# Local attention: softmax weights divided before they are turned, outputs made with features on partitions

## The chip, the cores and the metric

The kernel runs on one core of a Trainium2 chip. The core has TensorE (PE in the profile; its weight loads are a row of their own, PEld), VectorE (DVE), ScalarE (ACT), GpSimd (POOL) and SyncE (SP, which here only issues DMAs). Each engine works through its own queue in order, and semaphores make one wait for another. TensorE's results go to PSUM, from which DVE and ACT read them; everything else lies in SBUF. The metric is the device time of one execution in microseconds.

## The reference

The program is a stack of two adaLN blocks on an input of 4 batches x 1024 tokens x 128 features, each block with an attention and a feed-forward part, all in float32. The second block's feed-forward part is itself a small transformer of two layers with local attention, and it is what the change touches. Of it this matters:

```python
q, k, v = split(shift_token(x) @ wqkv)           # 8 heads of 64
q, k = l2norm(q) * qs, l2norm(k) * ksc
q, k = rotary_xpos(q, k)
bq = q.reshape(b, h, w, 64, d) * 8.0             # windows of 64 queries
bk, bv = look_around(k), look_around(v)          # 128 keys: the window before and this one
sim = einsum('bhwid,bhwjd->bhwij', bq, bk)
sim = where((i < j) | (i > j + 64) | (j == -1), -max, sim)
attn = softmax(sim, axis=-1)
out = einsum('bhwij,bhwjd->bhwid', attn, bv)
x = x + out @ wo
x = x + (a * gelu(g)) @ w2 + b2                  # after a layer norm and x @ w1
```

## The kernel before, in words

Earlier stages (the first block, the second block's windowed attention) fill the first 668 us or so and are not touched. The last stage, from line 786 on, makes the small transformer: 2 layers x 4 batches x 8 tiles of 128 tokens, 64 tiles in one loop, `g` counting them. A tile holds two windows of 64 queries. Features lie on partitions for the residual stream (`yT`, `xT`, `hs`), tokens for everything between the projections and the turned weights.

The work on a tile is spread over several rounds of the loop:

- `project` (L796, two rounds ahead): one matmul each for q and k (`qk`), the squares and their sums (`sq` on ACT, `ss` on DVE), the rotary products `co` and `si` on DVE, and on POOL `co + si` (L819), the inverse norm by a power (L818) and, for k, its product (L821).
- `turn` (L824, one round ahead): four transposes of q or k (`qktr`), copied to `qT` by ACT (L832) or into the batch's `kT` by DVE (L838).
- `values` (L840): v = h @ wv, copied by ACT (L847) to a tile of 8 heads x 65 columns whose last column POOL sets to one (L846); two DMAs of 64 partitions each make `ve`, the same values one window earlier.
- `scores` (L856): the mask goes into PSUM by a matmul (L863), the scores of the tile are added (L873), DVE takes the negative maxima (L877) and scales them by q's inverse norm (L878), and ACT writes exp (L882), eight instructions of 128 columns, with scale and bias as per-partition operands. The `j` of all these functions is a head's half: head 2c + j.
- `flip` (L885, one round later): four transposes of the weights per `j` (`ptr`, L890), copied to `pt` by ACT (L892).
- `outputs` (L895, two rounds later), per `j`: eight matmuls of 65 columns with the turned weights as the stationary operand (L903). Column 64 is the sum of the exps, by the column of ones. DVE takes its reciprocal (L905) and multiplies the 64 feature columns by it (L908). Queries are on partitions.
- `back` (L910, three rounds later): four transposes (L916) put features on partitions, and ACT copies them to `os` (L920).
- `project_out` (L922): every four tiles, `os` times `wo`, added to `yT` by DVE (L928).

The MLP of an earlier group of four tiles is cut into side jobs (L947 to L981: shift, layer norm in and out, gate, up, down) that a table hands to particular rounds. A gate, an up or a down job is three matmuls of 512 columns.

PE's queue is written by hand: the loop at the end of the stage calls these functions in the order in which PE is to do them. The other engines' queues are put in order by the framework's scheduler. PSUM has two banks for scores (`pS`) and six for everything else (`pM`); a matmul into one of the six waits until the last reader of what lay there is done. `pr` and `pt` have four buffers each.

Of the kernel before, what the change touches and what calls it, by code (L numbers as in the profile page):

```python
# [19 lines left out]
F32 = mybir.dt.float32  # L20
BF16 = mybir.dt.bfloat16
AF = mybir.ActivationFunctionType
ALU = mybir.AluOpType
# [3 lines left out]
P = 128  # L27
B, N, D = 4, 1024, 128
NT = N // P
BLK = 512  # L30
# [6 lines left out]
HEADS, DH, DEPTH = 8, 64, 2  # L37
# [11 lines left out]
def adaln_blocks(ctx: ExitStack, tc: tile.TileContext, a: dict, out: bass.AP):  # L49
    nc = tc.nc  # L50
    pe, act, dve, pool = nc.tensor, nc.scalar, nc.vector, nc.gpsimd
# [4 lines left out]
    def const(name, shape, dtype=F32):  # L56
        return cp.tile(shape, dtype, tag=name, name=name)
# [5 lines left out]
    def bc(ap, shape):  # L63

        return ap.unsqueeze(len(ap.shape)).to_broadcast(shape)
# [35 lines left out]
    ident = const("ident", [P, P])  # L101
# [10 lines left out]
    with tc.tile_pool(name="modps", bufs=2, space=PSUM) as mp:  # L112
        sc = const("sc", [P, 2, B])
        act.activation(sc, cT, AF.Silu)
        for blk in range(2):
            ps = mp.tile([P, 6, B], F32, tag="mod", name=f"modps{blk}")
# [92 lines left out]
    ps = both.enter_context(tc.tile_pool(name="ps", bufs=1, space=PSUM))  # L209
# [94 lines left out]
    with (  # L304
# [7 lines left out]
        kept = {}  # L312
# [325 lines left out]
    with (  # L638
# [61 lines left out]
        def outputs(b, t):  # L700

            O = ps.tile([P, 4, P], F32, tag="o", name=f"o_{b}_{t}")
            kept1["go"] = O
            for x in range(2):
                for g in range(2):
                    pe.matmul(
                        O[64 * g : 64 * g + 64, x, :], lhsT=hm64 if x else kept1[b, "vg"][:, g, :], rhs=kept1[b, t, "pg"][:, g, :],
                        start=(x == 0), stop=False, skip_group_check=True,
                    )
            cs = [c for c in range(4 * t - 2, 4 * t + 4) if c >= 0]  # L710
            for c in cs:
                lo, hi = max(c * KB, t * P), min(c * KB + W3, (t + 1) * P)
                for x in range(2):
                    for j in range(4):
                        pe.matmul(  # L715
                            O[32 * j : 32 * j + 32, x, lo - t * P : hi - t * P],
                            lhsT=hm32 if x else kept1[b, c // 4, "v"][:, 4 * (c % 4) + j, :],
                            rhs=kept1[b, c // 4, "p", j][:, c % 4, lo - c * KB : hi - c * KB],
                            start=False, stop=(c == cs[-1]), skip_group_check=True,
                        )  # L720
            if t % 4 == 0:
                kept1[b, t // 4, "os"] = wb.tile([P, BLK], F32, tag="os", name=f"os_{b}_{t}")
            os = kept1[b, t // 4, "os"]
            rs = wp.tile([P, P], F32, tag="rs", name=f"rs_{b}_{t}")
            dve.reciprocal(rs, O[:, 1, :])
            dve.tensor_tensor(os[:, (t % 4) * P : (t % 4 + 1) * P], O[:, 0, :], rs, ALU.mult)
# [24 lines left out]
        def when(g, f, *args):  # L751
            if 0 <= g < NG8:
                f(*divmod(g, NT), *args)

        for g in range(NG8 + 2):
            b, t = divmod(g, NT)
# [30 lines left out]
    with (  # L787
# [6 lines left out]
        kept = {}  # L794
# [45 lines left out]
        def values(l, b, t):  # L840

            nt = f"{l}_{b}_{t}"
            ps = pM.tile([P, BLK], F32, tag="mid", name=f"v_{nt}")
            pe.matmul(ps, lhsT=hs[l, b][:, t * P : (t + 1) * P], rhs=wl[l][0][:, 2, :], start=True, stop=True)  # L844
            v = wp.tile([P, HEADS, DH + 1], F32, tag="v", name=f"vs_{nt}")
            pool.memset(v[:, :, DH : DH + 1], 1.0)  # L846
            act.copy(v[:, :, 0:DH], ps.rearrange("p (h e) -> p h e", e=DH))  # L847
            ve = wp.tile([P, HEADS, DH + 1], F32, tag="ve", name=f"ve_{nt}")
            if t == 0:
                pool.memset(ve[0:64], 0.0)  # L850
            else:
                nc.sync.dma_start(out=ve[0:64], in_=kept[l, b, t - 1, "v"][64:128])
            nc.sync.dma_start(out=ve[64:128], in_=v[0:64])
            kept[l, b, t, "v"], kept[l, b, t, "ve"] = v, ve

        def scores(l, b, t):  # L856

            nt = f"{l}_{b}_{t}"
            q, k = kept[l, b, t, "q"], kept[l, b, "k"]
            S = [pS.tile([P, 4, P], F32, tag="s", name=f"s_{nt}_{j}") for j in range(2)]  # L860
            for j in range(2):
                rw = slice(64 * j, 64 * j + 64)
                pe.matmul(S[j], lhsT=rep64[rw, :], rhs=mkl[rw, :].unsqueeze(1).to_broadcast([64, 4, P]), start=True, stop=False)  # L863
            if t == 0:
                for j in range(2):
                    rw = slice(64 * j, 64 * j + 64)
                    pe.matmul(S[j][0:64, :, 0:64], lhsT=rep64[rw, 0:64], rhs=neg64[rw, :].unsqueeze(1).to_broadcast([64, 4, 64]), start=False, stop=False)
            for c in range(4):
                for e in range(2):
                    for j in range(2):  # L870
                        rw, qs = slice(64 * j, 64 * j + 64), slice(64 * e, 64 * e + 64)
                        at = (2 * t + e) * 64
                        pe.matmul(S[j][qs, c, :], lhsT=q[rw, c, qs], rhs=k[rw, c, at : at + P], start=False, stop=(c == 3))  # L873
            mx = wp.tile([P, 2, 4], F32, tag="mx", name=f"mx_{nt}")
            rq = kept[l, b, t, "ss"][:, 0, :].rearrange("p (c j) -> p j c", j=2)
            for j in range(2):
                dve.tensor_reduce(mx[:, j, :], S[j], AX.X, ALU.max, negate=True)  # L877
                dve.tensor_tensor(mx[:, j, :], mx[:, j, :], rq[:, j, :], ALU.mult)  # L878
            for j in range(2):
                pr = wp.tile([P, 4, P], F32, tag="pr", name=f"pr_{nt}_{j}", bufs=4)  # L880
                for c in range(4):
                    act.activation(pr[:, c, :], S[j][:, c, :], AF.Exp, bias=mx[:, j, c : c + 1], scale=rq[:, j, c : c + 1])  # L882
                kept[l, b, t, "pr", j] = pr

        def flip(l, b, t, j):  # L885
# [6 lines left out]
            act.copy(pt, tp)  # L892
            kept[l, b, t, "pt", j] = pt

        def outputs(l, b, t, j):  # L895
            nt = f"{l}_{b}_{t}_{j}"
            pt = kept.pop((l, b, t, "pt", j))
            o = pM.tile([P, BLK], F32, tag="mid", name=f"o_{nt}")
            o = o[:, 0 : 4 * (DH + 1)].rearrange("p (h e) -> p h e", e=DH + 1)
            for c in range(4):  # L900
                for e, vv in ((0, kept[l, b, t, "ve"]), (1, kept[l, b, t, "v"])):
                    qs = slice(64 * e, 64 * e + 64)
                    pe.matmul(o[qs, c, :], lhsT=pt[:, c, qs], rhs=vv[:, 2 * c + j, :], start=True, stop=True)  # L903
            rs = wp.tile([P, 4, 1], F32, tag="rs", name=f"rs_{nt}", bufs=4)
            dve.reciprocal(rs, o[:, :, DH : DH + 1])  # L905
            if j == 0:
                kept[l, b, t, "o"] = wp.tile([P, 4, 2, DH], F32, tag="on", name=f"on_{nt}", bufs=2)
            dve.tensor_tensor(kept[l, b, t, "o"][:, :, j, :], o[:, :, 0:DH], rs.to_broadcast([P, 4, DH]), ALU.mult)  # L908

        def back(l, b, t):  # L910

            nt = f"{l}_{b}_{t}"
            on = kept.pop((l, b, t, "o"))
            tp = pM.tile([P, 4, P], F32, tag="mid", name=f"otr_{nt}")
            for c in range(4):
                pe.transpose(tp[:, c, :], on[:, c, :, :].rearrange("p j e -> p (j e)"), ident)  # L916
            i = t % 4
            if i == 0:
                kept[l, b, t // 4, "os"] = wb.tile([P, 4, BLK], F32, tag="os", name=f"os_{nt}")
            act.copy(kept[l, b, t // 4, "os"][:, :, i * P : (i + 1) * P], tp)  # L920

        def project_out(l, b, k):  # L922
            s = slice(k * BLK, (k + 1) * BLK)
# [78 lines left out]
        for l in range(DEPTH):  # L1002
            for b in range(B):
                g = (l * B + b) * NT
# [18 lines left out]
        for g in range(-2, tiles + 12):  # L1023
            side = steps.get(g, [])
            when(g, scores)
            when(g + 2, project, 0)
            when(g - 1, flip, 0)
            when(g + 2, project, 1)
            when(g - 1, flip, 1)
            when(g + 1, turn, 0)  # L1030
            when(g - 2, outputs, 0)
            for f, args in side[:1]:
                f(*args)
            when(g + 1, turn, 1)
            when(g - 2, outputs, 1)
            when(g, values)
            when(g - 3, back)

            f0 = g - 7 if g < tiles - 2 else g - 6
            if f0 % 4 == 0 and 0 <= f0 < tiles and g != tiles - 1:  # L1040
                project_out(f0 // (B * NT), f0 // NT % B, f0 % NT // 4)
            for f, args in side[1:]:
                f(*args)
# [148 lines left out]
```

## Time and profile before

| | us |
|---|---|
| median of 3 runs | 1399.29 (1398.83 to 1407.56) |
| the profiled execution | 1399.1 |
| its span on the core | 1397.3 |
| last stage's first score matmul for tile 0 | 669.2 after the span's start |
| eight tiles, 1087.41 to 1175.47 | 88.06 |

The page of the profile gives, for each engine, busy time with its share of the span and the number of instructions, and the groups of instructions by line with mean durations and with the idle time ahead of them. Matmuls are pipelined, so PE's busy time counts overlapping work once, and the distance between the starts of two matmuls tells more than their durations. A float32 matmul shows as two rows. The granted TensorE clock over the span is 0.982 of full speed, and 1.00 in the last stage from 700 us on.

### The profile page before, as it was taken

How to read it: one execution, taken by the hardware profiler on the slowest of the kernel's cores; microseconds unless marked ns; L12 is line 12 of the kernel's file. 1: busy time of each engine (PE TensorE's matmuls, PEld its weight loads, DVE VectorE, ACT ScalarE, POOL GpSimd, SP SyncE). 2: the span in 40 equal slices, each digit the busy share in tenths (PEclk: the TensorE clock that was granted, in tenths of full speed). 3: DMA queues.
4: the chain of work that ended last, by engine and by line, in shares of the span. 5: the costliest groups of instructions: out<-in, count | busy, mean ns of one | idle time of the engine just before them, and what ended most of it. 6: DMA issues, size and time to landing. Idle time of an engine off the chain costs nothing.

```text
span 1397.3 us, 33849 instructions
## 1 busy us (share of the span) xinstructions
PE 1311.6 (94%) x13908; PEld 810.3 (58%) x13908; DVE 885.1 (63%) x2090; ACT 702.8 (50%) x1453; POOL 730.6 (52%) x750
## 2 busy tenths in 40 slices
PE   5799988997999999998899999999999999999997
PEld 4544544444777677676466566656666566666553
DVE  5655444523555555554788778877788777887753
ACT  2463532321222222222576776767667776677752
POOL 4454537461232405211987676666767667766620
PEclk9799999998999999999899999999999999999999
DMA  6031221213000000000111111111211111111111
GB/s 180 0 123 55 68 67 57 69 53 121 3 3 3 17 3 18 3 3 3 24 33 45 38 43 32 24 43 33 48 34 25 43 32 43 44 35 36 40 35 30
DMA packets 38655, 56.14 MB, mean 40 GB/s; under 512 B 6331, under 2 KB 18661, under 8 KB 38373
## 3 DMA queue, kind: packets, MB, share of 16 engines
q1 hardware_dynamic: 37204, 52.44, 14.1%
q8 instruction: 110, 1.80, 0.5%
q10 hardware_dynamic: 1296, 1.54, 0.3%
q14 instruction: 45, 0.36, 0.1%
HBM read 27.24 MB, written 2.36 MB: 21 GB/s over the span
## 4 chain that ended last, share of the span: by engine, by line
PE 77%; DVE 8%; POOL 7%; ACT 3%; issue 3%; DMA 1%; POOLq 0%; ACTq 0%; SPq 0%
PE qk L802 7%; PE v L844 4%; PE o L903 4%; PE s L873 4%; PE t L677 4%; PE yp L927 4%; PE qktr L829 4%; PE ptr L890 3%; PE o L715 3%; PE gm L961 3%; PE h L494 3%; PE a L970 3%; PE ym L978 3%; PE vp L653 3%; POOL u L498 2%
## 5 line engine op out<-in xcount | busy, mean ns | idle before, releaser
L819 POOL TENSOR_TENSOR co<-co,si 128x512 f32<-128x512 f32 x128 | 162.7, 1273 | 129.1 <-DVE si L812 128.7
L818 POOL TENSOR_TENSOR ss<-ss,nhalf 128x16 f32<-128x16 f32 x64 | 187.2, 2925 | 4.7
L882 ACT ACTIVATE pr<-s,mx,ss 128x128 f32<-128x128 f32 x512 | 186.5, 480 | 1.8
L805 ACT ACTIVATE sq<-qk 128x512 f32<-128x512 f32 x128 | 79.5, 621 | 171.7 <-PE qk L802 98.1
L802 PE MATMUL qk<-wqkv,hs 128*128 128x512 f32 x256 | 137.2, 620 | 0.8 <-DVE xT L732 0.8
L498 POOL TENSOR_TENSOR u<-u,cw 128x512 f32<-128x512 f32 x64 | 81.1, 1270 | 93.2 <-ACT u L497 74.5
L494 PE MATMUL h<-hT,w 128*128 128x512 f32 x256 | 122.1, 597 | 1.6 <-DVE g L500 1.6
L877 DVE TENSOR_REDUCE mx<-s 128x4 f32<-128x512 f32 x128 | 82.3, 684 | 56.1 <-PE s L873 56.0
L500 DVE TENSOR_TENSOR g<-u,h 128x512 f32<-128x512 f32 x64 | 43.7, 685 | 114.8 <-POOL u L498 112.6
L285 DVE TENSOR_REDUCE mx<-s 128x4 f32<-128x448 f32 x128 | 70.9, 616 | 70.4 <-PE s L282 70.4
L680 ACT ACTIVATE pt<-t 128x384 f32<-128x384 f32 x128 | 55.8, 488 | 116.9 <-PE t L677 116.9
L650 POOL COPY hr<-hT 128x512 f32<-128x512 f32 x32 | 19.5, 614 | 176.4 <-PE vp L653 172.3
L807 DVE TENSOR_TENSOR co<-qk,ab 128x512 f32<-128x512 f32 x128 | 87.7, 685 | 28.6 <-ACT sq L805 28.3
L890 PEld LDWEIGHTS ptr<-ident,pr 128*128 128x128 f32 x512 | 63.6, 141 | 64.8 <-issue 53.4
L829 PE MATMUL qktr<-ident,co 128*128 128x128 f32 x512 | 78.1, 275 | 11.5 <-POOL co L821 10.5
L497 ACT ACTIVATE u<-h 128x512 f32<-128x512 f32 x64 | 38.3, 598 | 97.3 <-PE h L494 90.4
L903 PE MATMUL o<-vs,pt 128*64 128x65 f32 x1024 | 86.9, 228 | 0.0
L812 DVE TENSOR_TENSOR si<-qk,ab 128x512 f32<-128x512 f32 x128 | 86.8, 678 | 0.0
L903 PE MATMUL o<-ve,pt 128*64 128x65 f32 x1024 | 86.6, 227 | 0.0
L814 DVE TENSOR_REDUCE ss<-sq 128x8 f32<-128x512 f32 x128 | 86.2, 673 | 0.0
L494 PEld LDWEIGHTS h<-hT,w 128*128 128x128 f32 x256 | 47.8, 192 | 61.9 <-issue 53.5
L903 PEld LDWEIGHTS o<-ve,pt 128*64 128x64 f32 x1024 | 69.2, 137 | 23.1 <-issue 16.1
(234 smaller groups left out, 3060.6 us busy)
## 6 DMA issues: line engine op xcount, KB each, us to landing
cw<-cd SPq DMA_DIRECT2D x128, 128.0 KB, 3.1
ve<-vs SPq DMA_DIRECT2D x120, 130.0 KB, 2.3
hs_m<-hT SPq DMA_DIRECT2D x24, 128.0 KB, 2.2
xin<-in_x SPq DMA_DIRECT2D x4, 512.0 KB, 6.9
hs<-hT SPq DMA_DIRECT2D x8, 256.0 KB, 2.9
out<-out SPq DMA_DIRECT2D x8, 256.0 KB, 2.5
hs<-hT SPq DMA_DIRECT2D x8, 255.8 KB, 3.7
w<-in_w SPq DMA_DIRECT2D x3, 512.0 KB, 5.0
```

The lines of the kernel that those rows point to most:

```text
L494: pe.matmul(h, lhsT=w[:, c * P : (c + 1) * P], rhs=hT[b][:, blk(k)], start=True, stop=True)
L498: pool.tensor_tensor(u, u, kept[b, k, "cw"][:, c, :], ALU.mult)
L802: pe.matmul(ps, lhsT=hs[l, b][:, t * P : (t + 1) * P], rhs=wl[l][0][:, w, :], start=True, stop=True)
L807: dve.tensor_tensor(co, ph, abs_[l][:, 0, t, w, :].unsqueeze(1).to_broadcast([P, HEADS, DH]), ALU.mult)
L812: dve.tensor_tensor(si.rearrange("p h (i e) -> p h i e", i=2), ex, sn, ALU.mult)
L814: dve.tensor_reduce(ss[:, w, :], sq, AX.X, ALU.add)
L818: pool.tensor_tensor(ss, ss, nhalf[:, 0:2].unsqueeze(2).to_broadcast([P, 2, HEADS]), ALU.pow)
L819: pool.tensor_tensor(co, co, si, ALU.add)
L829: pe.transpose(tp[:, i, :], co[:, i * P : (i + 1) * P], ident)
L882: act.activation(pr[:, c, :], S[j][:, c, :], AF.Exp, bias=mx[:, j, c : c + 1], scale=rq[:, j, c : c + 1])
L890: pe.transpose(tp[:, c, :], pr[:, c, :], ident)
L903: pe.matmul(o[qs, c, :], lhsT=pt[:, c, qs], rhs=vv[:, 2 * c + j, :], start=True, stop=True)
```

## The change

The division by the sum of the exps moves from the outputs to the weights, ahead of their turning, and the outputs are made with the values as the stationary operand, so that their features come out on partitions.

- `values` makes tiles of 64 columns a head; the column of ones and its memset are gone.
- `scores` asks each exp for the sum along its row (`accum_out`), takes the reciprocals on DVE and multiplies the weights by them in place, per `j`.
- `outputs` makes both `j` in one call: 16 matmuls of 64 columns with `v` or `ve` as the stationary operand and the turned weights as the moving one, into one PSUM tile, which ACT copies to `os`.
- `back` is gone, and with it the four transposes of a tile.
- In the loop, the outputs stand after the first side job and ahead of the second `turn`. In the order that the scheduler makes for DVE, the two reciprocals and two products stand behind `ss` of the round's q projection and ahead of `co` of its k projection; the kT copy stands behind that projection in most rounds, and behind the first product in the rounds that hold `project_out`.

```diff
-            v = wp.tile([P, HEADS, DH + 1], F32, tag="v", name=f"vs_{nt}")
-            pool.memset(v[:, :, DH : DH + 1], 1.0)
-            act.copy(v[:, :, 0:DH], ps.rearrange("p (h e) -> p h e", e=DH))
-            ve = wp.tile([P, HEADS, DH + 1], F32, tag="ve", name=f"ve_{nt}")
+            v = wp.tile([P, HEADS, DH], F32, tag="v", name=f"vs_{nt}")
+            act.copy(v, ps.rearrange("p (h e) -> p h e", e=DH))
+            ve = wp.tile([P, HEADS, DH], F32, tag="ve", name=f"ve_{nt}")
...
+            sm = wp.tile([P, 2, 4], F32, tag="sm", name=f"sm_{nt}")
             for j in range(2):
                 pr = wp.tile([P, 4, P], F32, tag="pr", name=f"pr_{nt}_{j}", bufs=4)
                 for c in range(4):
-                    act.activation(pr[:, c, :], S[j][:, c, :], AF.Exp, bias=mx[:, j, c : c + 1], scale=rq[:, j, c : c + 1])
+                    act.activation(
+                        pr[:, c, :], S[j][:, c, :], AF.Exp, bias=mx[:, j, c : c + 1], scale=rq[:, j, c : c + 1], accum_out=sm[:, j, c : c + 1]
+                    )
+                dve.reciprocal(sm[:, j, :], sm[:, j, :])
+                dve.tensor_tensor(pr, pr, bc(sm[:, j, :], [P, 4, P]), ALU.mult)
                 kept[l, b, t, "pr", j] = pr
...
-        def outputs(l, b, t, j):
-            nt = f"{l}_{b}_{t}_{j}"
-            pt = kept.pop((l, b, t, "pt", j))
-            o = pM.tile([P, BLK], F32, tag="mid", name=f"o_{nt}")
-            o = o[:, 0 : 4 * (DH + 1)].rearrange("p (h e) -> p h e", e=DH + 1)
+        def outputs(l, b, t):
+
+            nt = f"{l}_{b}_{t}"
+            pt = [kept.pop((l, b, t, "pt", j)) for j in range(2)]
+            o = pM.tile([P, 4, P], F32, tag="mid", name=f"o_{nt}")
             for c in range(4):
                 for e, vv in ((0, kept[l, b, t, "ve"]), (1, kept[l, b, t, "v"])):
                     qs = slice(64 * e, 64 * e + 64)
-                    pe.matmul(o[qs, c, :], lhsT=pt[:, c, qs], rhs=vv[:, 2 * c + j, :], start=True, stop=True)
-            rs = wp.tile([P, 4, 1], F32, tag="rs", name=f"rs_{nt}", bufs=4)
-            dve.reciprocal(rs, o[:, :, DH : DH + 1])
-            if j == 0:
-                kept[l, b, t, "o"] = wp.tile([P, 4, 2, DH], F32, tag="on", name=f"on_{nt}", bufs=2)
-            dve.tensor_tensor(kept[l, b, t, "o"][:, :, j, :], o[:, :, 0:DH], rs.to_broadcast([P, 4, DH]), ALU.mult)
-
-        def back(l, b, t):
-
-            nt = f"{l}_{b}_{t}"
-            on = kept.pop((l, b, t, "o"))
-            tp = pM.tile([P, 4, P], F32, tag="mid", name=f"otr_{nt}")
-            for c in range(4):
-                pe.transpose(tp[:, c, :], on[:, c, :, :].rearrange("p j e -> p (j e)"), ident)
+                    for j in range(2):
+                        pe.matmul(o[64 * j : 64 * j + 64, c, qs], lhsT=vv[:, 2 * c + j, :], rhs=pt[j][:, c, qs], start=True, stop=True)
             i = t % 4
             if i == 0:
                 kept[l, b, t // 4, "os"] = wb.tile([P, 4, BLK], F32, tag="os", name=f"os_{nt}")
-            act.copy(kept[l, b, t // 4, "os"][:, :, i * P : (i + 1) * P], tp)
+            act.copy(kept[l, b, t // 4, "os"][:, :, i * P : (i + 1) * P], o)
...
             when(g + 1, turn, 0)
-            when(g - 2, outputs, 0)
             for f, args in side[:1]:
                 f(*args)
+            when(g - 2, outputs)
             when(g + 1, turn, 1)
-            when(g - 2, outputs, 1)
             when(g, values)
-            when(g - 3, back)
```

## The prediction

> **What bounds the kernel now.** I read the page first, then the busy time of one whole batch of the last stage (eight tiles), then the groups of that stage, then the timeline of single tiles.
>
> ```profile
> PE 1311.6 (94%) x13908; PEld 810.3 (58%) x13908; DVE 885.1 (63%) x2090; ACT 702.8 (50%) x1453; POOL 730.6 (52%) x750
> ...
> 1087.41:1175.47 88.06, 87.84 (x807) 53.43 (x807) 69.18 (x149) 61.36 (x132) 60.04 (x59) 1.00 0.16 36
> ```
>
> In the second line the columns are the stretch, its length, then busy time of PE, PEld, DVE, ACT, POOL, then granted clock. PE has work at every moment of the 88.06 us, DVE for 79% of them. Tiles come in a pattern of four, named here by their PE side job, with these distances between first score matmuls (L873): gate 10.5 (1131.80 to 1142.32), up 10.95 (1098.32 to 1109.27), down 10.52 (1109.27 to 1119.79), projection 12.01 (1119.79 to 1131.80). Their sum is 44.0; the stretch from 750 to 1344 holds 54 tiles at this pace. So PE's queue paces the stage. But how far behind is DVE? The last thing that a tile's scores need is the kT copy (L838), which DVE does at the end of its round:
>
> ```profile
> 1131.80 1.10 PE L873 MATMUL s<-kT,qT 64*64 64x128 f32 x32
> ...
> 1134.68 0.69 DVE L807 TENSOR_TENSOR co<-qk,ab 128x512 f32<-128x512 f32 x1 [0.24 <-ACT sq L805]
> ...
> 1138.46 0.69 DVE L807 TENSOR_TENSOR co<-qk,ab 128x512 f32<-128x512 f32 x1 [1.02 <-ACT sq L805]
> ...
> 1140.26 0.68 DVE L838 COPY kT<-qktr 128x512 f32<-128x512 f32 x1
> ```
>
> ```profile
> 1135.02 2.92 ACT L882 ACTIVATE pr<-s,mx,ss 128x128 f32<-128x128 f32 x8
> 1137.77 0.66 ACT L805 ACTIVATE sq<-qk 128x512 f32<-128x512 f32 x1
> 1138.24 0.66 ACT L892 COPY pt<-ptr 128x512 f32<-128x512 f32 x1
> ```
>
> Each line is a start, a length, and the instruction with what ended its engine's idle time. This is a gate tile. DVE's second co waits for sq, which stands behind the eight exps on ACT. kT ends at 1140.94, and the next scores start at 1142.32: 1.3 us to spare after 0.1 for the handing over. In the up tile kT ends at 1109.21 and the scores start at 1109.27: nothing to spare. In the down tile kT ends at 1119.27, scores start at 1119.79: 0.4 to spare.
>
> **What the change removes.** The groups of 750 to 1400 us (busy us and mean ns of one after the first bar):
>
> ```profile
> L882 ACT ACTIVATE pr<-s,mx,ss 128x128 f32<-128x128 f32 x440 | 160.3, 479 | 1.7
> ...
> L908 DVE TENSOR_TENSOR on<-o,rs 128x256 f32<-128x256 f32 x115 | 48.5, 421 | 3.4
> ...
> L916 PE MATMUL otr<-ident,on 128*128 128x128 f32 x232 | 34.9, 273 | 0.0
> ...
> L905 DVE RECIPROCAL rs<-o 128x4 f32<-128x4 f32 x114 | 19.7, 173 | 10.5 <-PE o L903 10.3
> ```
>
> PE loses four transposes (L916) a tile. Their place in the queue is 1107.98 to 1108.42, or 0.53 ahead of the masks: 0.44 to 0.53 us, so 64 x 0.5 = 32 us of PE. The output matmuls stay 16 of 64 columns instead of 65; one start of a group goes, under 0.1 us. DVE loses two reciprocals and two 128x256 multiplies, about 1.1 us of queue a tile, but they lie in holes: those of the first head half stand between ss and the wait for sq (1136.79 to 1137.43), those of the second half behind kT. Neither is ahead of kT on the path. POOL loses a 0.11 us memset from an idle stretch: nothing. The evacuation of v becomes contiguous (612 ns row, same size), and the os copy keeps its 620 ns; both free. What is moved: the first half's outputs go behind the first side job, with no DMA of theirs, and on ACT the os copy goes ahead of v's copy. That puts v 0.6 later, and v and its two DMAs (2.3 us) are read two tiles on: free, with some 20 us of cover.
>
> **What it adds.** (1) Two reciprocals (0.17, and 0.22 to the next start) and two 128x512 multiplies with both inputs in SBUF. The nearest row is L359, 0.67 to 0.69 us alone; back to back such instructions start every 0.60 to 0.65. The built order puts all four ahead of the second co, and in gate, up and down tiles kT stands behind that co, si and ss. (2) Accumulation in 512 exps. No row shows it. Summing can't shorten an exp, so from below nothing; from above the smallest ACT row, sc 128x8 at 209 ns, if each sum is an instruction of its own. Exps of 480 start every 0.35, so they overlap by 0.12 to 0.13, and such an instruction would add 0.08 to 0.21. [...] I take 0.09 each: 0.72 for eight. (3) The reciprocal waits for four exps and sits at the head of DVE's queue; co, si, ss, kT, and so PE's next scores, wait behind it.
>
> [...] A DVE multiply with both inputs in SBUF meets POOL:
>
> ```profile
> 880.23 1.04 POOL L821 TENSOR_TENSOR co<-co,ss 128x512 f32<-128x512 f32 x1
> ...
> 880.50 0.86 DVE L878 TENSOR_TENSOR mx<-mx,ss 128x4 f32<-128x4 f32 x2
> ```
>
> L878 takes 0.15 alone; here the first takes 0.79, ending with L821. At 166.32, L359 takes 1.43 beside L498. [...] the pair of L878 at 698.18 runs in 0.28 inside an L818 that lasts from 697.24 to 700.16. I go by the row: L819 (1.27), L821 (1.04) and L150 (1.04) block, L818 does not. [...]
>
> **Tile by tile**, in us from the tile's first score matmul.
> Gate: the exps end at 6.14 now, 6.86 then. The second multiply starts at 7.1, co at 7.75 instead of 6.66, kT ends at 10.2. PE, which lost 0.5, is later than that: the built waits let the output matmuls start only when the second pt copy has freed its PSUM bank (7.10, then 7.85), followed by 1.2 of outputs (now in one piece), 0.52 qktr, 0.96 v, 0.33 masks: 10.85. Cost +0.3 (-0.4 with free sums, +1.3 with 0.21).
> Up: the three ge of the MLP end on DVE at 7.9 (8.5 now: the matmuls start 0.6 earlier, no first outputs ahead of them). Then 0.65 + 0.2 + 0.65 of the new work, then co, si, ss, kT, 2.4 as now: scores at 11.9. Cost +0.95 (+1.7 with 0.21).
> Down: layer-norm work on DVE starts the round 0.55 earlier than now (the second multiply behind kT is gone). First multiply at 5.4, second ready at 7.2 when the exps are done; POOL's L149, L150, L819 run from 4.9 to 8.4, so it starts at 7.2 or behind L819 at 8.4. hT and kT follow: +0.6 or +1.8, I take +1.2.
> Projection: kT stands behind the first multiply only, but v now waits for that copy with nothing between qktr and v (outputs stood there): v at 7.4, yp at 8.4 against 8.16 now: +0.2 (+0.9 with 0.21).
> Sum: 2.65 per four tiles, x 13.5 = +36. The ten tiles before 750, where kT stands early and POOL's L821 paced the round, grow by about 0.6 each, as the first multiply waits for L819 there: +6. The profiled execution took 1399.1 (span 1397.3, 1.8 around it), within 0.2 of the median of the runs. **1399.1 + 42 = 1441.**
>
> **The rivals.** *PE's relief decides* (faster): PE has 94% of the span and 77% of the chain of waits, and the removed 0.5 a tile would all come off. Against: the score matmuls need kT, whose spare time is 1.3, 0 and 0.4 us, and the new DVE pieces are 1.25 even if nothing waits. It decides only if those add less than some 0.4 ahead of kT, on the mean. 1399 - 32 = 1367. Chance 0.08. *Nearly even*: kT's delay and PE's gain cancel, 1388 to 1412: 0.09. *Cheap sums[...]*: per four tiles -0.4 + 0.95 + 0.55 + 0.2 = 1.3, x 13.5 = 18, and 4: 1421 (1412 to 1428), chance 0.2. *Dear sums*: 0.21 each: 1.3 + 1.7 + 1.85 + 0.9 = 5.75, x 13.5 = 78, and 8: 1485 (1468 to 1490), chance 0.15. *The forecast*, 1428 to 1468: 0.48.
>
> **The numbers.** One per cent, 14 us, is what a measurement can tell from no change. Faster 0.08, same 0.10 (with a little of the cheap case), slower 0.82. The range 1408 to 1480 leaves out the faster case, part of the even one and the end of the dear one.
>
> **What would show it.** PE no longer without a gap: score matmuls (now L872) waiting for DVE kT, most in up and down tiles, 0.5 to 2 us each. Exps eight in 3.6 us instead of 2.92. The new multiply's mean well over 0.69, with values up to 1.9 where POOL's L819 or L150 runs. A batch of eight tiles at 93 us instead of 88. A batch under 87 would make me wrong about kT; exps at 2.92 or above 4.5, about the sums.

## The result, and the profile after

| | before | after |
|---|---|---|
| median of 4 runs, us | 1399.69 (1398.83 to 1407.56) | 1463.76 (1460.60 to 1469.95) |
| span of the profiled execution | 1397.3 | 1464.4 |
| first score matmul of tile 0 | 669.2 | 677.8 |
| from there to the end of the span (the last stage) | 728.1 | 786.6 |

The change is slower: the ratio is 1.0447, with an interval of 1.0413 to 1.0481. The forecast was 1441, range 1408 to 1480.

Of the 67.1 us between the two profiled spans, 8.6 lie ahead of the last stage, in programs that the change does not touch (the granted clock was lower there, 0.74 against 0.87 from 320 to 360 us for one); runs of one kernel differ by about as much (before: 1398.83 to 1407.56). From here on the length of the last stage is compared: +58.5.

The first line of the page, after:

```profile
PE 1294.0 (88%) x13652; PEld 786.2 (54%) x13652; DVE 927.3 (63%) x2090; ACT 747.6 (51%) x1965; POOL 729.1 (50%) x686
```

PE was busy 1311.6 us before and is busy 17.6 less, in a span that is 67 longer: it waits now. Four tiles (gate, up, down, projection), each from its first score matmul to that of the next; columns as in the prediction (stretch, length, busy time of PE, PEld, DVE, ACT, POOL, granted clock, then the DMA's share and GB/s):

```profile
1041.65:1052.42 10.77, 9.81 (x98) 5.67 (x97) 8.30 (x16) 8.44 (x24) 5.63 (x6) 1.00 0.18 39
1052.42:1064.11 11.69, 10.21 (x101) 6.07 (x99) 9.66 (x20) 10.10 (x28) 6.41 (x5) 1.00 0.11 25
1064.11:1076.01 11.90, 9.76 (x94) 5.72 (x95) 10.51 (x25) 7.13 (x23) 9.43 (x11) 1.00 0.16 36
1076.01:1089.68 13.67, 12.89 (x101) 7.52 (x101) 8.44 (x16) 7.70 (x24) 7.62 (x6) 0.88 0.11 24
```

Before they took 10.5, 10.95, 10.52 and 12.01. The last one is the surprise. Its granted clock is 0.88, where every tile at this pace had 1.00 before, and it is not always so: of the 13 projection tiles from tile 11 on, 4 take 12.03 to 12.05 us, as before, and 8 take 13.6 to 13.7 at 0.88; tile 11 takes 13.23 at full clock (12.62 before). The down tile that comes ahead of it, its beginning and its end, from the timeline (start, length, instruction, idle time and what ended it):

```profile
1064.11 1.10 PE L872 MATMUL s<-kT,qT 64*64 64x128 f32 x32 [1.48 <-DVE kT L838]
...
1069.97 1.06 POOL L150 TENSOR_TENSOR xh_m<-xh_m,rv_m 128x512 f32<-128x512 f32 x1
...
1070.99 0.18 DVE L885 RECIPROCAL sm<-sm 128x4 f32<-128x4 f32 x1 [0.86 <-ACT pr L882]
1070.99 1.27 POOL L819 TENSOR_TENSOR co<-co,si 128x512 f32<-128x512 f32 x1
...
1071.20 1.61 DVE L886 TENSOR_TENSOR pr<-pr,sm 128x512 f32<-128x512 f32 x1
...
1072.74 0.68 DVE L807 TENSOR_TENSOR co<-qk,ab 128x512 f32<-128x512 f32 x1
...
1075.19 0.68 DVE L838 COPY kT<-qktr 128x512 f32<-128x512 f32 x1
...
1076.01 0.90 PE L872 MATMUL s<-kT,qT 64*64 64x128 f32 x13 [2.14 <-DVE kT L838]
```

The second multiply is ready at 1071.20, just after POOL's L819 has begun, and lasts 1.61 us; the next DVE piece starts 1.54 after it. Then co, si, ss, hT and kT follow, and PE has nothing to do for 2.14 us. The clock around that gap, in stretches (columns as above):

```profile
1072.00:1073.87 1.87, 1.87 (x12) 0.79 (x8) 1.87 (x3) 1.18 (x3) 0.27 (x1) 1.00 0.00 0
1073.87:1076.01 2.14, 0.00 (x0) 0.03 (x1) 2.00 (x4) 0.30 (x1) 1.68 (x3) 1.00 0.31 68
1076.01:1079.40 3.39, 3.39 (x34) 2.17 (x35) 1.52 (x3) 0.00 (x0) 3.31 (x2) 0.53 0.16 34
1079.40:1084.00 4.60, 4.60 (x55) 3.44 (x53) 3.44 (x7) 4.11 (x17) 1.77 (x2) 0.98 0.01 4
```

PE is empty in the second stretch, and in the 3.4 us after it the clock is about one half (0.50 in the middle of the stretch), for scores and q/k projections. That costs 1.64 us (13.67 against the 12.03 of a tile that keeps its clock). The groups from 750 to 1400 us (busy us, mean ns of one, idle time before):

```profile
L882 ACT ACTIVATE pr<-s,mx,ss 128x128 f32<-128x128 f32 x440 | 195.3, 475 | 0.4 <-DVE mx L877 0.2
...
L882 ACT ACTIVATION_READ_ACCUMULATOR pr<-s,mx,ss 128x1 f32 x440 | 97.4, 221 | 0.0
L886 DVE TENSOR_TENSOR pr<-pr,sm 128x512 f32<-128x512 f32 x110 | 91.1, 828 | 2.8
...
L872 PE MATMUL s<-kT,qT 64*64 64x128 f32 x1757 | 64.9, 286 | 49.6 <-DVE kT L838 47.6 <-ACT qT L832 2.0
```

Each sum is an instruction of its own, 221 ns, on ACT. It overlaps its exp, so that the distance between two exps grows from 343 to 435 ns: 0.092. The score matmuls wait 47.6 us for the kT copy. In gate tiles kT is not what ends last: as the prediction had it, the outputs wait there for the second pt copy, 0.96 us.

```profile
1049.57 0.34 PE L908 MATMUL o<-pt,ve 128*64 128x64 f32 x4 [0.96 <-ACT pt L896]
```

### The profile page after: what moved, and what is told of

The parts are those of the page before. It is cut to its first block, busy times and chain, and to the rows that moved or that the text cites. A ratio compares the mean times of both kernels' runs of the same rounds, so it can differ in the third digit from the quotient of the medians.

```text
span 1464.4 us, 33751 instructions
## 1 busy us (share of the span) xinstructions
PE 1294.0 (88%) x13652; PEld 786.2 (54%) x13652; DVE 927.3 (63%) x2090; ACT 747.6 (51%) x1965; POOL 729.1 (50%) x686
## 3 DMA queue, kind: packets, MB, share of 16 engines
q10 hardware_dynamic: 1296, 1.54, 0.3%
HBM read 27.24 MB, written 2.36 MB: 20 GB/s over the span
## 5 line engine op out<-in xcount | busy, mean ns | idle before, releaser
L819 POOL TENSOR_TENSOR co<-co,si 128x512 f32<-128x512 f32 x128 | 163.6, 1279 | 232.2 <-DVE si L812 202.4
L882 ACT ACTIVATE pr<-s,mx,ss 128x128 f32<-128x128 f32 x512 | 227.3, 475 | 0.6 <-DVE mx L877 0.4
L818 POOL TENSOR_TENSOR ss<-ss,nhalf 128x16 f32<-128x16 f32 x64 | 189.3, 2957 | 5.3
L802 PE MATMUL qk<-wqkv,hs 128*128 128x512 f32 x256 | 148.6, 667 | 0.8 <-DVE xT L732 0.8
L872 PE MATMUL s<-kT,qT 64*64 64x128 f32 x2048 | 77.5, 292 | 56.8 <-DVE kT L838 54.6
L882 ACT ACTIVATION_READ_ACCUMULATOR pr<-s,mx,ss 128x1 f32 x512 | 113.5, 222 | 0.0
L894 PEld LDWEIGHTS ptr<-ident,pr 128*128 128x128 f32 x512 | 66.7, 147 | 75.8 <-issue 61.2
L886 DVE TENSOR_TENSOR pr<-pr,sm 128x512 f32<-128x512 f32 x128 | 105.3, 823 | 3.1
L872 PEld LDWEIGHTS s<-kT,qT 64*64 64x64 f32 x2048 | 61.3, 142 | 73.2 <-issue 69.1
L829 PE MATMUL qktr<-ident,co 128*128 128x128 f32 x512 | 80.8, 281 | 15.2 <-POOL co L821 14.2
```

The source lines that it names most:

```text
L818: pool.tensor_tensor(ss, ss, nhalf[:, 0:2].unsqueeze(2).to_broadcast([P, 2, HEADS]), ALU.pow)
L819: pool.tensor_tensor(co, co, si, ALU.add)
L829: pe.transpose(tp[:, i, :], co[:, i * P : (i + 1) * P], ident)
L886: dve.tensor_tensor(pr, pr, bc(sm[:, j, :], [P, 4, P]), ALU.mult)
L894: pe.transpose(tp[:, c, :], pr[:, c, :], ident)
```

## The experiments

The theory: DVE and ACT work ahead of the kT copy makes the scores late (up and down tiles most); in the down tile POOL's L819 holds the second multiply up on top of that (1.61 us beside it, 0.69 with POOL idle); PE's idle time there then halves its clock (0.50 behind the gap of 2.14 us). The rivals: the new order of PE's queue costs; the sums alone cost; the multiplies' waiting for the exps is the path, wherever kT stands.

| run | last stage, us | gate, up, down, projection, us |
|---|---|---|
| before | 728.1 | 10.52, 10.95, 10.52, 12.01 |
| after | 786.6 | 10.77, 11.69, 11.90, 12.03 or 13.67 |
| e1 no division | 705.1 | 10.03, 10.63, 9.92, 11.95 |
| e2 k turned early | 753.0 | 10.37, 10.47, 11.60, 11.86 |
| e3 useless matmuls | 776.8 | 10.77, 11.69, 11.82, 12.03 |
| e4 sums alone | 739.2 | 10.76, 11.36, 10.23, 12.03 |
| e5 squares later | 758.9 | 10.30, 11.05, 11.74, 12.2 or 13.1 to 13.7 |
| e6 and k turned earlier | 762.7 | 10.55, 11.05, 11.74, 12.2 or 13.1 to 13.9 |
| e7 scalar form | 800.1 | 10.76, 12.14, 12.79, 12.03 |
| e8 no sums | 742.2 | 9.98, 11.46, 10.65, 11.95 |
| e9 layer norm's product on ACT | 844.9 | 10.77, 11.69, 15.23, 12.0 to 13.3 |
| e10 e5 and e9 | 799.6 | 10.30, 11.06, 14.2, 12.22 |
| e11 before, with sums | 742.5 | 10.95, 10.95, 10.78, 12.02 |
| e12 that product left out | 760.0 | 10.77, 11.69, 10.98, 12.03 |

The last stage runs from its first score matmul to the end of the span in each profile; the four distances are those of the pattern in the middle of the stage. There is one profile of each kernel, so a stage's length is that of one execution; the times and ratios below are of several.

**What each part costs: e1, e4, e8, e11.** e1 drops the accumulation, the reciprocals and the multiplies:

```diff
-  act.activation(pr[:, c, :], ..., scale=rq[:, j, c : c + 1], accum_out=sm[:, j, c : c + 1])
+  act.activation(pr[:, c, :], ..., scale=rq[:, j, c : c + 1])
-  dve.reciprocal(sm[:, j, :], sm[:, j, :])
-  dve.tensor_tensor(pr, pr, bc(sm[:, j, :], [P, 4, P]), ALU.mult)
```

> The changed kernel without its division: no accumulated sums, no reciprocals, no multiplies; the order of PE's queue and the form of the outputs stay. The weights are not normalised, so the outputs aren't the reference's. Theory (the added DVE and ACT work ahead of the kT copy costs the time, and PE's idle time ahead of the projection tile's scores halves its clock on top): with that work gone kT is early enough, PE has no idle stretch of 2 us, the granted clock of the batches is 1.00 and four tiles take about 43 us: 1378 us (1365 to 1392). Rival (the order costs: outputs in one piece behind the side job, waiting for both pt copies): 1420 us or more, with idle time ahead of the output matmuls.

Measured: 1383.56 us (1375.12 to 1384.11), ratio to before 0.985 (0.981 to 0.990). A batch of eight tiles of e1:

```profile
1075.27:1160.30 85.03, 81.99 (x779) 48.37 (x777) 57.98 (x118) 61.25 (x132) 59.66 (x51) 1.00 0.16 37
```

Against 88.06 before, with the clock at 1.00. The new order, the four transposes fewer and the old division gone from DVE are together a gain, 23 us of the stage; no run separates them. The rival of the order is out.

e4 keeps the accumulation and drops the two DVE lines:

> The changed kernel with the accumulated sums taken by the exps, but no reciprocals and no multiplies (the sums are not used, so the outputs aren't normalised). Theory: eight exps with their sums take 3.65 us instead of 2.92, which costs about 0.3 us a tile: 1395 us (1380 to 1410), between e1 and the changed kernel and much nearer to e1. Rival (the sums carry most of the loss): 1430 to 1460 us.

Measured: 1413.11 us (1411.29 to 1422.45), ratio 1.010 (1.006 to 1.014). That is above the expected range and short of the rival's. The stage grows by 34.1 over e1, where I had expected about 17: gate and up tiles by 0.73 each, the full length of the eight sums, the down tile by 0.3, and late in the stage more.

e8 is the changed kernel with its multiplies, but without the accumulation:

```diff
-  dve.reciprocal(sm[:, j, :], sm[:, j, :])
+  dve.reciprocal(sm[:, j, :], pr[:, :, 64])
```

> The changed kernel without the accumulation: the reciprocal is taken of one column of the exps (which waits for the same four exps) instead of their sums, so the division is by wrong numbers; multiplies stay. Theory: exps go back from 3.65 to 2.92 us for eight; if the prices of sums (34 us between e1 and e4) and multiplies add, 1430 us (1418 to 1442). Rival (sums only matter because the multiplies wait for them, so that their price with the multiplies is above that without): under 1415 us.

Measured: 1413.62 us (1412.71 to 1422.10), ratio 1.010 (1.006 to 1.013). The number is the rival's; its reason holds in part. The sums cost 34.1 us of the stage by themselves (e4 less e1), reciprocals and multiplies 37.1 (e8 less e1), both 81.5 (after less e1): 10 more than their sum. The two do add up to more in the down tile: 9.92 in e1, +0.31 with sums, +0.73 with multiplies, +1.98 with both. In the up tile they add up to less: 10.63, +0.73, +0.83, +1.06. And the eight projection tiles at 0.88 of the clock make 13.1 of after's 81.5, where e4 has one such tile and e8 none: the 10 us are no more than what the clock took. One part of e8 differs from after besides the sums: in projection tiles its kT copy stands at the end of DVE's round, and those tiles take 11.95 all the same.

e11 adds the sums to the kernel before, where nothing reads them:

> The kernel before with the accumulated sums added to its exps and nothing else; nothing reads them. Theory: eight exps take 3.65 instead of 2.92 us; the gate tile has 1.3 us to spare and loses nothing, the up tile has none and loses 0.7, the down tile 0.3, the projection tile 0.1: 1.1 per four tiles, 1414 us (1406 to 1424). Rival (the sums cost as much in the old order as in the new one, 34 us): 1428 to 1438 us.

Measured: 1414.15 us (1412.91 to 1422.48), ratio 1.010 (1.006 to 1.014): +14.4 us of the stage, as expected, though not where: the gate tile, which I thought safe with its 1.3 us to spare, lost 0.43, and the up tile nothing. So the same sums cost 14 us in a queue whose PE has work left to do, and 34 in one that has less: from 760 to 1340 us the score matmuls wait 2.3 us for kT in e11, 24.9 in e4.

**The clock: e3.** Two matmuls that nothing reads fill PE's gap ahead of the projection tiles:

```diff
+  if g % 4 == 2 and 0 <= g < tiles - 1:
+      fl = pM.tile([P, BLK], F32, tag="mid", name=f"fl_{g}")
+      for _ in range(2):
+          pe.matmul(fl, lhsT=ident, rhs=hs[g // (B * NT), g // NT % B][:, 0:BLK], start=True, stop=True)
```

> The changed kernel with two useless 128x512 matmuls on PE at the end of every fourth round, in the gap of 2.1 us ahead of the masks and scores of a projection tile; nothing reads them. Theory (PE's idle time there halves its clock for about 3.5 us): the granted clock of the batches goes back to 1.00, the slow projection tiles (13.7 us from score to score) become 12.1, and some 9 of them x 1.65 come off: 1448 us (1442 to 1453). Rival (the clock falls for another reason, or its fall costs nothing): 1460 us or more, and slow projection tiles as before.

Measured: 1451.97 us (1448.56 to 1456.59), ratio 1.035 (1.030 to 1.040). Timeline of PE at the end of a down tile:

```profile
1069.78 1.88 PE L1037 MATMUL fl<-hs,ident 128*128 128x512 f32 x4
1071.60 0.39 PE L862 MATMUL s<-masks 64*128 64x512 bf16 x2
1072.32 1.10 PE L872 MATMUL s<-kT,qT 64*64 64x128 f32 x32 [0.33 <-DVE kT L838]
```

The down tile is as long as before the edit (11.82), since it waits for kT; but 0.33 us of the gap is left, the clock stays up (1.00 from 1038.05 to 1130.67, two tiles of each kind), and all 13 projection tiles take 12.03 to 12.05. Work that does nothing made the kernel 12 us faster. The first eight tiles, where other rounds have gaps, stayed slow (85.8 us, 83.9 in after).

Why did the clock stay up behind the same gap ahead of four of twelve projection tiles? In the traces of before and after, any two changes of the granted clock lie a whole number of steps of 3.413 us apart, to 0.002 us; in after it falls at 932.85, 980.64, 1028.42 and 1076.21, 14 steps from each to the next. What sets the steps no run shows. Here are two neighbouring steps, counted off from these, around a gap of 2.14 us, once ahead of tile 19 (gap from 883.37) and once ahead of tile 35 (gap from 1073.87):

```profile
881.65:885.06 3.41, 1.71 (x8) 0.66 (x8) 3.41 (x6) 1.33 (x3) 1.43 (x3) 1.00 0.08 17
885.06:888.48 3.42, 2.97 (x40) 2.06 (x41) 1.88 (x6) 0.73 (x2) 3.26 (x3) 1.00 0.27 59
...
1072.80:1076.21 3.41, 1.27 (x12) 0.33 (x14) 3.06 (x6) 0.69 (x2) 1.88 (x3) 1.00 0.25 56
1076.21:1079.62 3.41, 3.41 (x34) 1.97 (x28) 1.74 (x3) 0.00 (x0) 3.33 (x2) 0.50 0.10 21
```

The first gap is cut in two by the border between the steps, and PE is busy for 0.50 of one step and 0.87 of the next: the clock stays. The second lies within one step, PE is busy for 0.37 of it, and the next step runs at half. So it is throughout the last stage of after: each of the thirteen full-clock steps with PE busy for 0.18 to 0.37 is followed by half clock, and none with 0.42 or more. In the last stage of before, the two with 0.18 and 0.40 are followed by it, and none with 0.64 or more. Ahead of the last stage the two traces show no such clean border: in before a step with 0.76 was followed by half clock, one with 0.41 was not.

**POOL and the multiply: e12, and e9, which missed.** e12 leaves out POOL's L150 in the last stage, so that L819 begins a microsecond sooner:

```diff
-        pool.tensor_tensor(xh, xh, rv.to_broadcast([P, 4, D]), ALU.mult)
+        if not skip:
+            pool.tensor_tensor(xh, xh, rv.to_broadcast([P, 4, D]), ALU.mult)
```

> The changed kernel without that POOL step (L150, 1.04 us in each down tile) at all: the last stage's layer norms are not divided by the deviation, so the outputs aren't the reference's; every other engine's queue is as in the changed kernel. POOL starts the down tile's L819 a microsecond earlier. Theory (L819 shuts out the second multiply of the down tile, kT is late by that, PE idles for 2.1 us and its clock halves): that multiply falls from 1.62 to 0.7 us, down tiles from 11.9 to 11.0, projection tiles 12.05 throughout: 1437 us (1428 to 1447). Rival (the second multiply is not what kT waits for, or another POOL instruction takes L819's place): down tiles above 11.6, 1455 us or more.

Measured: 1431.62 us (1430.08 to 1439.07), ratio 1.022 (1.019 to 1.025). DVE, and then POOL, in a down tile of e12:

```profile
1060.31 0.18 DVE L886 RECIPROCAL sm<-sm 128x4 f32<-128x4 f32 x1 [0.85 <-ACT pr L883]
1060.52 0.69 DVE L887 TENSOR_TENSOR pr<-pr,sm 128x512 f32<-128x512 f32 x1
1061.13 0.68 DVE L808 TENSOR_TENSOR co<-qk,ab 128x512 f32<-128x512 f32 x1
```

```profile
1059.19 1.39 POOL L820 TENSOR_TENSOR co<-co,si 128x512 f32<-128x512 f32 x1
```

L820, which is L819 in after, ends at 1060.58, and the multiply behind it takes 0.69 instead of 1.61. Down tiles fall from 11.90 to 10.98, the gap to 1.2 us, and every projection tile from tile 15 on takes 12.03 to 12.05: 26.6 us of the stage hang on eighteen POOL instructions of one microsecond, about half of it through the clock.

e9 was meant to show the same with the product kept, as four pieces on ACT:

> The changed kernel with one POOL step of the last stage's layer norm (L150, xh times the inverse deviation, 128x512, 1.04 us in each down tile) done on ACT in four pieces of 128 columns. In the down tile POOL then starts L819 a microsecond earlier. Theory (POOL's L819 shuts out the down tile's second multiply, which makes kT late by 1 us, which makes PE idle for 2.1 us and halves its clock): no multiply of a down tile above 1.2 us, down 11.9 to about 11.0, the slow projection tiles become 12.05, clock 1.00 from 760 us on: 1437 us (1428 to 1447). Rival (the down tile waits for something else, or ACT's four pieces make the exps late by as much): above 1455 us.

Measured: 1515.07 us (1514.10 to 1519.28), ratio 1.082 (1.077 to 1.087). ACT in a down tile:

```profile
1078.02 1.28 ACT L154 ACTIVATE xh_m<-xh_m,rv_m 128x128 f32<-128x128 f32 x4 [6.88 <-POOL rv_m L149]
1079.21 0.57 ACT L809 ACTIVATE sq<-qk 128x512 f32<-128x512 f32 x1
1079.68 0.44 ACT L886 ACTIVATE pr<-s,mx,ss 128x128 f32<-128x128 f32 x1
```

The pieces wait for POOL's L149 at the head of ACT's queue, with sq and the exps behind them, and down tiles take 15.23. The number is the rival's. This says nothing on POOL and the multiply; it says what a misplaced wait costs. e10 joins it to e5 and fails in the same way, outside both of its expectations:

> e5 and e9 together: k's squares behind its rotary products, and the layer norm's product on ACT. Theory: the down tile's two multiplies, 1.27 and 1.55 us in e5, fall to 0.7 to 1.1, down 11.74 becomes 10.8, projection 12.2 throughout; four tiles take 44.3 instead of 45.3 to 46.8: 1410 us (1398 to 1422). Rival (e5's multiplies in down tiles are shut out by L819 wherever it lies): within 8 us of e5.

Measured: 1477.61 us (1470.23 to 1483.40), down tiles 14.2.

**Another form of the multiply: e7.**

```diff
-  dve.tensor_tensor(pr, pr, bc(sm[:, j, :], [P, 4, P]), ALU.mult)
+  for c in range(4):
+      dve.tensor_scalar(pr[:, c, :], pr[:, c, :], sm[:, j, c : c + 1], None, ALU.mult)
```

> The changed kernel with each 128x512 multiply by broadcast reciprocals written as four 128x128 multiplies by a per-partition scalar, which have one large input in SBUF instead of two. Theory (an instruction with two inputs in SBUF is shut out by POOL's L819, L821 and L150; mean 0.82 instead of 0.69, up to 1.62 in down tiles): the four pieces together take about 0.7 to 0.9 us, none of them waits for POOL, down tiles fall from 11.9 to about 11.2 and the other tiles change by less than 0.2: 1452 us (1440 to 1462). Rival (pieces of this form are shut out too, or cost over 0.25 each): 1465 us or more.

Measured: 1471.14 us (1470.73 to 1471.84), ratio 1.049 (1.044 to 1.053), on the rival's side. The group from 750 to 1400 us:

```profile
L887 DVE TENSOR_SCALAR pr<-pr,sm 128x128 f32<-128x128 f32 x436 | 118.2, 337 | 2.3
```

Set beside POOL's timeline over the whole run, the pieces take 0.28 us with POOL idle (404 of them) and 0.72 where they overlap an L819 alone (42). So one large input in SBUF does not spare an instruction the delay. But the down tiles' 12.79 is not that delay alone. The gap is now ahead of the down tiles, 1.93 us, and in 10 of the 12 from tile 14 to tile 58 the clock falls behind it:

```profile
1109.59 1.10 PE L872 MATMUL s<-kT,qT 64*64 64x128 f32 x32 [1.93 <-DVE kT L838]
```

```profile
1111.08:1114.49 3.41, 3.41 (x8) 1.65 (x7) 3.06 (x8) 1.93 (x6) 3.17 (x4) 0.50 0.01 2
```

The two down tiles that kept their clock take 12.20 and 12.21: the form costs 0.3, the clock 0.6.

**DVE's order: e2, e5, e6.** e2 moves k's turning directly behind q's:

> The changed kernel with k's turning (qktr and the kT copy) moved from behind the outputs to directly behind q's, ahead of the side job; the kT copy then stands ahead of the new multiplies in DVE's queue in most rounds. Theory (kT behind the multiplies is the path): score matmuls stop waiting for kT, the clock stays at 1.00 and the time falls under that of the kernel before, 1380 us (1365 to 1400). Rival (the later exps on ACT are the path, whatever the order of DVE, because the outputs wait for the second pt copy): 1420 to 1450 us.

Measured: 1431.94 us (1427.12 to 1432.83), ratio 1.020 (1.016 to 1.024): 32 us better than after, but far from the 1380 of the theory. What waits in e2, from 760 to 1400 us (total us, times, longest):

```profile
PEld qktr L829 <- POOL co L821: 49.4, 37, 4.0
...
PE qktr L829 <- POOL co L821: 39.6, 28, 3.8
```

By the number this is the rival's side, but not by its wait. kT no longer ends last; L821 does. POOL's power (2.92) and L821 (1.04) start only when the round before has given ss, and k's transposes, now early in PE's queue, stand there and wait, 1.64 us in a down tile:

```profile
1052.16 0.66 PE L829 MATMUL qktr<-ident,co 128*128 128x128 f32 x4 [1.64 <-POOL co L821]
```

I had not looked at that wait when I moved the step past it.

e5 takes k's squares after its rotary products, so that co and si of k need no longer wait for ACT (DVE's co waited 12.3 us for sq from 750 to 1400 us in after) and run during the exps:

```diff
-  act.activation(sq, ph, AF.Square)
+  if w == 0:
+      act.activation(sq, ph, AF.Square)
 ...
   dve.tensor_tensor(si.rearrange("p h (i e) -> p h i e", i=2), ex, sn, ALU.mult)
+  if w == 1:
+      act.activation(sq, ph, AF.Square)
```

> The changed kernel with one statement moved: for k, the squares (sq, ACT) are taken after the rotary products (co, si, DVE) instead of before them. The two read the same PSUM tile, and the reader that comes second in the program waits for the first; so co of k no longer waits for sq, which stands behind the eight exps on ACT, and DVE does co and si during the exps. Theory (kT is late because co, si, ss and the multiplies all queue up on DVE after the exps' end): after the exps only two short and two long pieces and ss stand ahead of kT, 1.2 us less in gate and down tiles; up 11.0, down 10.8, no idle stretch of 2 us ahead of the projection tile, clock 1.00: 1415 us (1402 to 1430). Rival (the multiplies' waiting for the sums is itself the path): no more than 10 us gained, 1450 us or above.

Measured: 1432.98 us (1430.24 to 1442.56), ratio 1.023 (1.017 to 1.030). Up tiles fell to 11.05, as expected, and gate tiles to 10.30; down tiles, expected at 10.8, stayed at 11.74. DVE in one of them:

```profile
1044.13 1.27 DVE L889 TENSOR_TENSOR pr<-pr,sm 128x512 f32<-128x512 f32 x1
1045.33 0.17 DVE L888 RECIPROCAL sm<-sm 128x4 f32<-128x4 f32 x1
1045.53 1.55 DVE L889 TENSOR_TENSOR pr<-pr,sm 128x512 f32<-128x512 f32 x1
```

With co early on DVE, the two sums of L819 (L822 in e5) came one behind the other on POOL, and both multiplies ran into them:

```profile
1043.58 2.95 POOL L822 TENSOR_TENSOR co<-co,si 128x512 f32<-128x512 f32 x2
```

The 31 us gained over after are more than the 10 that this rival allowed, and e2's 32 say the same: the multiplies' waiting for the exps is not by itself the path. e6 turns k ahead of the outputs as well:

> As e5, and in PE's queue k's turning ahead of the outputs instead of behind them, still behind the side job. Theory: the outputs' wait for the second pt copy (gate tiles) and the turning change places, the kT copy comes ahead of the last multiply where it can; gate 10.3, up 10.7, down 10.5, projection 12.0: 1405 us (1385 to 1420), under the kernel before only if kT no longer ends last in any tile. Rival: in most tiles DVE keeps kT behind the second multiply, so as e5 within 5 us.

Measured: 1435.01 us (1434.99 to 1445.68), ratio 1.025 (1.019 to 1.030): as e5, on the rival's side.

None of the versions with the division beats the kernel before. Not tried: e5 with L150 out of POOL's way but not at the head of ACT's queue.

## Why the prediction was right, and where it was not

The sign, the range and the likeliest case held; 1464 is 23 over the forecast time. Of these 23, 16.5 lie in the last stage (+58.5 against +42), the rest ahead of it or in the scatter of the runs. By its own steps:

- **Tiles.** Gate +0.2 to +0.25 (forecast +0.3), up +0.74 (+0.95), down +1.38 (+1.2), projection at full clock +0.02 (+0.2): 46.4 for four, where the sum gave 46.65. The last 54 tiles grew by 44.4 us against 36. Of these the eight slow projection tiles make 13.1, counted over 12.04 each. So without the clock the term is 31, a little less than forecast; these 5 us too many hide part of the term that was missing, which is luck.
- **Sums.** 0.092 each, 0.09 taken, an estimate of mine inside the 0.08 to 0.21 that the rows of before gave. Eight exps and sums take 3.65 us, 3.6 forecast.
- **PE's relief.** e1 bears out that it is real (23 us of the stage, of 32 counted, with the old division on DVE gone as well), and after shows that it comes to nothing behind the kT copy. The rival that it decides is out.
- **kT.** Score matmuls wait for it, as forecast, 1.48 us ahead of a down tile and 2.14 ahead of a projection tile.
- **POOL and the multiply.** The prediction put the down tile's second multiply "at 7.2 or behind L819 at 8.4"; it started at 7.09 and ended at 8.70, 0.55 after L819. Beside L819 alone the multiplies take 1.11 us on the mean (34 of 128), beside L818 alone 0.69 (2), with POOL idle 0.69 (64). What the two engines share no run shows. That L818 does not hold DVE up, which the prediction read from one pair of L878, is borne out for these multiplies, on two cases; in e7 twelve of the small pieces beside L818 alone take 0.28, as with POOL idle, and in before L878 takes 0.16 on the mean beside L818 alone (35), as with POOL idle (30), against 0.43, and up to 1.00, beside L821 alone (57). L150 has one case in before: L359 takes 1.08 beside it, 0.69 with POOL idle. e12 gives the price: 0.92 of the down tile's 1.38.
- **What failed is the bold sum: it has no term for the clock.** The prediction expected PE to have gaps of 0.5 to 2 us and took a gap to cost its own length. In eight projection tiles a gap cost 1.64 more: 13.1 us, and e3, where every projection tile keeps its clock, shows the cause. In the ten tiles ahead of the 54, forecast at +6, the stage lost 14.1: there gaps of 3.34 and 3.65 us stand ahead of the scores of tiles 1 and 2, and the mean clock of the ten is 0.92 (0.97 before). PE runs at half clock for 12.7 us there, 5.5 before, which can make at most 3.6 of the 8.1 over forecast. So the missing term is about 13 us shown, and up to 5.3 argued from the clock alone (these 3.6, and 1.7 for a step at half clock in tile 10); what the rest of the 8.1 is stays open. These first gaps come with the multiplies: the ten tiles take 89.4 us in e1, 89.5 with sums alone (e4), 101.7 with multiplies alone (e8).
- **Also not counted:** that sums and multiplies together can cost more than apart, 0.94 in a down tile.

## What to carry to other kernels

When a change opens an idle stretch on PE, look at what the clock does behind it: a gap of 2.1 us cost its own length and, in eight tiles of twelve, 1.64 us more, and useless matmuls in it paid. Before a step is moved in an engine's queue, list the waits that it brings to its new place; three of the experiments failed by that (POOL's L821 in e2, L149 at the head of ACT's queue in e9 and e10). And price two additions to one chain together: in the down tile they cost nearly twice what they cost apart (1.98 against 0.31 and 0.73), in the up tile less.

## What the runs showed of the chip

- In after, gaps of 2.14 to 2.19 us ahead of the scores of projection tiles were followed by a granted clock of one half for 3.4 us in 8 of 12 cases, and so was one of 2.36 us ahead of tile 10; gaps of 1.48 us ahead of those of down tiles, 13 of them, in none. In e7, gaps of 1.93 us ahead of down tiles were followed by it in 10 of 12 cases. In the last stage of after, every full-clock step of 3.413 us in which PE was busy for 0.18 to 0.37 was followed by one at half clock (13), and none with 0.42 or more.
- A multiply of 128x128 by a per-partition scalar, with one large input in SBUF, was held up by POOL's additions like one of 128x512 with two: in e7 0.28 us with POOL idle, 0.72 on the mean beside L819 alone; in after 0.69 and 1.11.
- An accumulating exp issues a second ACT instruction, of 221 ns in after, of which 92 ns show: 435 ns from exp to exp, 343 before.
